# Two graph-attention layers on one core: the statistics of the last batch, one count, and the last normalization are moved

## The chip, the cores and the metric

The kernel runs on one core of one Trainium2 chip. The metric is the device time of one execution in microseconds (us): 3082.63 in the median of three runs, 3081.44 to 3082.72.

## The reference

For x of 16 x 1024 x 256 (float32) and 16 adjacency matrices of 1024 x 1024, two layers follow one another. Each layer normalizes, projects, attends under the mask of the adjacency matrix, projects back and adds to x:

```python
h = jnp.maximum(_layernorm(x), 0.0)
q, k, v = h @ Wq, h @ Wk, h @ Wv        # per head; layer 1 adds biases
scores = jnp.where(adj > 0, q @ k.T / sqrt(D), -inf)
heads = softmax(scores) @ v
x = x + concat(heads) @ Wo.T + bo
```

Layer 0 has 4 heads of 64 columns, layer 1 has 8 heads of 32.

## The kernel before

**Steps.** For one batch and one layer the queries are cut into two halves of 512 (`qh`), the heads into two groups (`g`), and the keys into tiles of 128. A *group* is one `qh` and one `g`; its work is a list of *steps*. A step computes four blocks of scores of 128 keys x 512 queries (`scores`), which fill two PSUM pairs. VectorE applies the mask while it reads each pair (`exponentials`, L562), ScalarE takes the exponential in place (L568), and two steps later (`LEAD`) TensorE multiplies the values by them (`weigh`, L580) into the PSUM tile `po`. A layer 0 group has 4 steps and a layer 1 group has 8. So a batch is 16 steps of layer 0 and 32 of layer 1, 768 steps over all batches. Layer 0 of batch b+1 stands before layer 1 of batch b. The text calls the first step of layer 1 of batch 14 (the last but one) c, as the code does; e = c + 32 is the first step of layer 1 of batch 15, and e + 31 is the last step of all.

**Sums.** The softmax needs the sum of the exponentials over the keys. In layer 1 GpSimd adds the tiles of an odd step to those of the even step before it (`count_steps`, L695, two adds). Accumulating DMAs on GpSimd's queue (`accumulate`, L681) add such tiles to each other. `count` (L425) then lets TensorE add over the partitions, with a matrix of ones, into the PSUM tile `pz`, which exists once. `halves` does a count as two counts of 256 columns in two following steps. After it `spread` (L445, L458) copies the sums to SBUF, into a tile of the tag inv, and sends them by four DMAs to a tile of 128 partitions; `invert` (L466, L468) takes reciprocals and writes them to DRAM; `fetch` (L477) reads them back, spread over partitions, into tiles of the tag inv, of which there are two; `normalize` (L485, GpSimd) multiplies the heads' output `cat`, which `copy_out` (L437, ScalarE) copied from `po`. `end_half` (L521, L526) multiplies by Wo and adds to x.

**Inputs of a layer.** `stats` (L198 and L199 on VectorE, then four small operations on GpSimd, L209 to L212) gives mean and variance of the four row tiles of a half; `norm` (L221, ScalarE) writes the normalized rows into the one tile of the tag hn; `add_bias` (L230, GpSimd) adds the output bias to x beforehand. `turn_blocks` (L273) transposes blocks of 32 x 32 on VectorE; `put_blocks` (L278) writes them to DRAM and `place_blocks` (L285, four DMAs) reads them back into hT. The products `k`, `q` (L307) and `values` (L383) read hT; each takes one of the three PSUM pairs that the scores use as well. ScalarE moves k and the values out of PSUM and VectorE moves q (L322).

**Order.** The order of every queue is the order in which `Stream.run` issues the work. It goes through the steps; `later(i, f, ...)` puts a piece of work into step i by hand. In a step come: the scores, the weighted values of the step two before, counts, the exponentials with the copies of finished groups between their halves, other due work in the order in which it was entered, and last the large products. At an even step of layer 1 that holds a large product, the weighted values are put off to the next step. `Group.waits` gives the step of a group's final count, counted from its end, and `end_group` the steps of spread, invert, fetch and normalize.

**The ends.** In the last 32 steps (`pairs`) every pair of steps is counted by itself. The last group (`hurry`) is counted at once, and `finish` ends the kernel: products of its half with Wo for the group before (L496), reciprocals of the sums straight from PSUM in two halves (L505), multiplication of `cat` by them (L506), the other products, the addition to x (L511) and the output DMAs (L514). `test` (L333, L336, GpSimd) then checks the sums' range; a reduction (L953) and a tiny product (L955) of its result follow, and a flag is read that selects a second program for inputs out of range.

Of the kernel before, what the change touches and what calls it, by code (L numbers as in the profile page):

```python
# [10 lines left out]
F32 = mybir.dt.float32  # L11
# [7 lines left out]
P = 128  # L19
# [71 lines left out]
def fast_program(ctx, tc, a, w, loads, chk):  # L91
# [5 lines left out]
    B, N, E = x.shape  # L97
    NT = N // P
# [5 lines left out]
    work = ctx.enter_context(tc.tile_pool(name="work", bufs=2))  # L104
# [288 lines left out]
    class Group:  # L393
# [93 lines left out]
        def finish(self):  # L487

            inp, qh = self.inp, self.qh
            inv = work.tile([P, 512], F32, tag="inv", name=f"inv_{self.n}")  # L490
            py = psum_pair(f"py_{self.n}").rearrange("p a (t e) -> p (a t) e", e=E)
            rows, cat = xs[inp.b, qh], self.half.cat
            dst = quarters(out, inp.b, qh)

            def product(i, c):
                nc.tensor.matmul(  # L496
                    py[:, i, :], cat[:, c, ts(i, P)], w.o[self.layer][:, c, :],
                    start=c == 0 and i % 2 == 0, stop=c == 1 and i % 2 == 1,
                )

            for i in range(4):
                product(i, 0)
            for h in range(2):
                q = ts(h, 256)
                nc.vector.reciprocal(tiled(inv)[:, ts(h, 2)], by_tile(self.s)[:, ts(h, 2)])  # L505
                nc.vector.tensor_mul(cat[:, self.g, q], cat[:, self.g, q], inv[:, q])  # L506
                for i in (2 * h, 2 * h + 1):
                    product(i, 1)
            for h in range(2):
                t = ts(h, 2)  # L510
                nc.vector.tensor_add(rows[:, t, :], py[:, t, :], rows[:, t, :])  # L511
                for g in range(4):
                    queue = nc.scalar if g % 2 else nc.sync
                    queue.dma_start(dst[g][:, t, :], rows[ts(g, 32), t, :])  # L514
# [91 lines left out]
    class Stream:  # L606
# [12 lines left out]
        def later(self, i, f, *args):  # L619
            self.due.setdefault(i, []).append((f, args))  # L620
# [5 lines left out]
        def run(self):  # L626
            steps = self.steps
            n = len(steps)
            waiting, i = [], 0
            while i < n + LEAD:  # L630
                wide = 2 if i < n and steps[i].gr.layer == 0 else 1
                span = range(i, i + wide)
                now = [steps[k] for k in span if k < n]
                waiting += [(k, steps[k - LEAD]) for k in span if k >= LEAD]
                for st in now:
                    scores(st)
                copies = []
                if wide == 2 or i % 2 or not self.large(i):
                    ahead = [st for _, st in waiting if st.gr.hurry and st.j >= NT - 2]
                    for _, st in waiting:  # L640
                        if st not in ahead:
                            weigh(st)
                    for k, st in waiting:
                        if st.gr.layer:
                            self.count_steps(k, st)
                        if st in ahead:
                            weigh(st)
                        if st.last:
                            copies.append(st.gr.copy_out)
                            self.end_group(k, st.gr)  # L650
                    waiting = []
                due = [self.due.pop(k, []) for k in span]

                for f, args in [e for of in due for e in of]:
                    if f.__name__ in COUNTS:
                        f(*args)
                for st in now:
                    exponentials(st, copies if wide == 1 else [])
                if not now:
                    for f in copies:  # L660
                        f()
                for k, of in zip(span, due):
                    if wide == 2 and k % 2:
                        for f in copies:
                            f()
                    if k % 2 and 3 <= k <= n and steps[k - 2].gr.layer == 0:
                        add_tiles(steps[k - 3], steps[k - 2])
                    for f, args in of:
                        if f.__name__ not in COUNTS and not self.rank((f, args)):
                            f(*args)  # L670
                for of in due:
                    for f, args in of:
                        if self.rank((f, args)):
                            f(*args)
                i += wide
            while self.due:
                for f, args in self.due.pop(min(self.due)):
                    f(*args)
# [4 lines left out]
        def count_steps(self, i, st):  # L683


            gr, j = st.gr, st.j
            if gr.hurry and j >= NT - 2:
                if st.last:
                    self.counted(i, gr)
                gr.count([of[:, r, :] for of in st.halves for r in range(2)], False, st.last)  # L690
            elif j % 2:
                one = self.steps[i - LEAD - 1].p
                for k, of in enumerate(st.halves):
                    half = one[:, ts(k, 2), :]
                    nc.gpsimd.tensor_add(half, half, of)  # L695
                if gr.pairs and (st.last or gr.hurry):
                    self.later(i + 2, gr.count, one, j == 1, st.last)
                elif gr.pairs:
                    self.halves(i + 3, gr, one, j == 1, False)
                elif j == 1:  # L700
                    gr.one = one
                elif gr.brief:
                    if j == 3:
                        self.accumulate(one, gr.one)
                        self.later(i + 6, gr.count, one, True, False)
                    elif j == 5:
                        self.halves(i + 5, gr, one, False, False)
                    else:
                        self.later(i + 4, gr.count, one, False, True)
                elif j == 5:  # L710
                    gr.two = one
                elif st.last and gr.qh and not gr.g:
                    self.accumulate(one, gr.two)
                    for k, of in enumerate((gr.one, one)):
                        self.later(i + gr.waits, gr.count, of, not k, k == 1)
                elif st.last and gr.last:
                    self.accumulate(gr.two, gr.one)
                    self.later(i + 1, self.accumulate, one, gr.two)
                    self.later(i + gr.waits, gr.count, one, True, True)
                elif st.last:  # L720
                    self.accumulate(gr.two, gr.one)
                    self.later(i + 2, self.accumulate, one, gr.two)
                    if gr.g:
                        self.halves(i + gr.waits, gr, one, True, True)
                    else:
                        self.later(i + gr.waits, gr.count, one, True, True)
                else:
                    self.accumulate(one, gr.one)
                    gr.one = one
# [12 lines left out]
        def end_group(self, i, gr):  # L742

            if gr.hurry:
                for f in (gr.spread, gr.finish, gr.inp.test):
                    self.later(i, f)
                return

            if gr.layer == 0:
# [5 lines left out]
                at = (3, 4, 5, 7, 13) if gr.qh else (3, 5, 6, 7, 11)  # L755
                if gr.inp.b == B - 1 and gr.qh:
                    at = 3, 6, 7, 9, 13
                if gr.inp.b == 0:
                    at = (2, 3, 4, 5, 8) if gr.qh else (3, 5, 6, 7, 9)
            else:  # L760
                at = ((9, 11, 13, 19), (8, 12, 14, 17, 19), (7, 9, 11, 14), None)[2 * gr.qh + gr.g]
                if gr.pairs:
                    at = 2, 5, 6, 7, 9
                elif gr.last:
                    at = 4, 6, 7, 9, 11
            for k, f in zip(at, (gr.spread, gr.invert, gr.fetch, gr.normalize)):
# [87 lines left out]
    later = stream.later  # L854
# [34 lines left out]
    for t in range(NT):  # L889
        i = 7 + 2 * t  # L890
# [8 lines left out]
    for b in range(B - 1):  # L899
# [32 lines left out]
                later(a + at[t + 1] + (1 if t == 4 else 2), mask.flip, t)  # L932
        else:
            last, e = inputs[1][b + 1], c + 32
            later(c + 5, last.stats, 0)
            later(c + 10, last.norm, 0)
            later(c + 13, last.add_bias, 0)
            block_inputs(last, 0, c + 11, c + 12, c + 13, c + 18, c + 22, c + 26)
            later(c + 18, last.stats, 1)
            later(c + 22, last.norm, 1)  # L940
            later(c + 23, last.add_bias, 1)
            block_inputs(last, 1, c + 23, c + 24, c + 26, e, e + 10, e + 2)
            for i, u in zip((4, 10, 14, 26, 36, 40, 42, 44), range(NT)):
                later(c + i, masks[b + 1].second, u)
    stream.run()

# [247 lines left out]
```

## Time and profile before

| what | us |
|---|---|
| median of three runs | 3082.63 |
| profiled execution, its own time | 3083.88 |
| its span, first to last instruction | 3082.1 |
| TensorE busy | 3061.3 |
| VectorE busy | 2464.4 |
| ScalarE busy | 2242.9 |
| GpSimd busy | 2462.1 |

PE is TensorE, PEld its weight loads, DVE VectorE, ACT ScalarE, POOL GpSimd, SP the queue of SyncE that issues most DMAs (SPq). A line of the timeline has the start, the time to the end of its last instruction, the engine, the line of the code, the operation, the output and inputs by the program's names, and the number of instructions merged in it; in brackets stands how long the engine idled before, and what ended that. A matmul of the program counts as two in the trace. A line of the windows has the stretch, its length, busy time and instructions of PE, PEld, DVE, ACT and POOL, the clock that TensorE was granted (1.00 is full), the share of the DMA engines in use, and GB/s.

### The profile page before, as it was taken

What the parts mean: (1) busy time and instruction counts of PE and PEld (TensorE: products, weight loads), DVE (VectorE), ACT (ScalarE), POOL (GpSimd) and SP (SyncE); (2) the same over time, 40 slices, a digit from 0 to 9 for tenths busy, and PEclk for the clock granted to TensorE, in tenths of its full rate; (3) what the DMA queues carried; (4) which work ended last, traced back from release to release, by engine and by line L of the source; (5) the groups of instructions that cost most, each with busy time, mean ns of one, the idle gap of its engine ahead of it and who ended that gap; (6) DMA issues with size and microseconds to landing.
All of it is one profiled execution on the core that took longest, in us unless ns stands there. A gap on an engine that the chain in (4) does not pass through costs nothing.

```text
span 3082.1 us, 46012 instructions
## 1 busy us (share of the span) xinstructions
PE 3061.3 (99%) x16678; PEld 1199.8 (39%) x16678; DVE 2464.4 (80%) x2712; ACT 2242.9 (73%) x2478; POOL 2462.1 (80%) x1584
## 2 busy tenths in 40 slices
PE   9999999999999999999999999999999999999998
PEld 4443433434334343343433334343343433434333
DVE  6778787887878878787887878878788787887877
ACT  5668777777777767777777777777777777776775
POOL 3578788787887878878788887888878778787886
PEclk9999999999999999999999999999999999999999
DMA  4226556464563645546456463654636546463431
GB/s 134 63 61 147 129 123 135 121 141 121 129 145 110 139 130 133 136 110 138 124 129 138 120 139 108 147 123 122 141 104 144 132 122 138 118 143 86 100 82 34
DMA packets 263548, 372.77 MB, mean 121 GB/s; under 512 B 58768, under 2 KB 218768, under 8 KB 242448
## 3 DMA queue, kind: packets, MB, share of 16 engines
q0 software_dynamic: 23472, 170.93, 28.2%
q1 hardware_dynamic: 239520, 198.56, 22.2%
q8 instruction: 133, 2.18, 0.3%
q14 instruction: 103, 0.84, 0.1%
q10 hardware_dynamic: 320, 0.26, 0.0%
HBM read 149.95 MB, written 47.96 MB: 64 GB/s over the span
## 4 chain that ended last, share of the span: by engine, by line
PE 92%; DVE 2%; DMA 2%; POOL 1%; issue 1%; SPq 1%; ACT 1%; DVEq 0%; ACTq 0%; POOLq 0%
PE ps L539 31%; PE po L580 28%; PE pq L307 10%; PE py L521 7%; PE pv L383 6%; PE pq L348 5%; PE pz L425 4%; PE pv L367 2%; DVE p L562 1%; DMA p<-p 1%; POOL p L695 1%; DMA sums<-s 0%; DMA inv<-vd 0%; ACT p L568 0%; SPq L458 0%
## 5 line engine op out<-in xcount | busy, mean ns | idle before, releaser
L562 DVE SCALAR_TENSOR_TENSOR p<-mask,ps 128x1024 f32<-128x1024 fp8e5 x1536 | 1791.6, 1215 | 346.0 <-PE ps L539 327.2
L568 ACT ACTIVATE p<-p 128x1024 f32<-128x1024 f32 x1536 | 1615.9, 1056 | 597.1 <-DVE p L562 535.4
L695 POOL TENSOR_TENSOR p<-p,p 128x1024 f32<-128x1024 f32 x510 | 1218.1, 2472 | 104.9 <-PE po L580 104.3
L539 PE MATMUL ps<-qT,kT 32*128 32x512 f32 (+1 forms) x6144 | 1089.9, 629 | 5.5 <-DVE p L562 3.5
L580 PE MATMUL po<-p,v 128*32 128x512 f32 (+1 forms) x6144 | 967.9, 599 | 0.4 <-ACT cat L437 0.4
L539 PEld LDWEIGHTS ps<-qT,kT 32*128 32x128 f32 (+1 forms) x6144 | 355.4, 184 | 640.2 <-DVE p L562 269.5
L580 PEld LDWEIGHTS po<-p,v 128*32 128x32 f32 (+1 forms) x6144 | 239.4, 118 | 669.7 <-issue 498.6
L593 POOL TENSOR_TENSOR p<-p 128x1024 f32<-128x1024 f32 x128 | 302.8, 2366 | 79.4 <-DVE p L592 74.1
L592 POOL TENSOR_TENSOR p<-p,p 128x1024 f32<-128x1024 f32 x64 | 151.2, 2363 | 157.3 <-DVE p L589 128.9
L485 POOL TENSOR_TENSOR cat<-cat,inv 128x512 f32<-128x512 f32 x127 | 175.2, 1383 | 77.7 <-DMA inv<-vd 76.5
L521 PE MATMUL py<-wo,cat 128*128 128x256 f32 x1008 | 234.4, 386 | 0.0
L521 PEld LDWEIGHTS py<-wo,cat 128*128 128x128 f32 x1008 | 186.3, 190 | 73.5 <-issue 16.7
L681 POOL DMA_DIRECT2D p<-p x163 | 144.8, 889 | 86.5 <-DMA p<-p 55.2
L383 PE MATMUL pv<-wv,hT 128*128 128x256 f32 x800 | 185.7, 385 | 0.0
L307 PE MATMUL pq<-hT,wq 128*128 128x512 f32 x400 | 184.8, 605 | 0.1
L167 ACT ACTIVATE mask<-adj,numbers 128x1024 fp8e5<-128x1024 int32 x128 | 145.9, 1140 | 45.0 <-DMA adj<-in_adj_dram 45.0
L383 PEld LDWEIGHTS pv<-wv,hT 128*128 128x128 f32 x800 | 148.0, 190 | 57.1 <-issue 25.2
L589 DVE TENSOR_TENSOR p<-p 128x1024 f32<-128x1024 f32 x128 | 166.9, 1304 | 0.0
L526 DVE TENSOR_TENSOR x<-py,x 128x1024 f32<-128x1024 f32 x63 | 77.1, 1224 | 109.1 <-PE py L521 109.1
L437 ACT COPY cat<-po 128x512 f32<-128x512 f32 x128 | 73.7, 576 | 118.5 <-PE py L521 96.6
L595 POOL TENSOR_TENSOR p<-p,p 128x1024 f32<-128x1024 f32 x64 | 151.9, 2373 | 5.0
L230 POOL TENSOR_TENSOR x<-x,bo 128x1024 f32<-128x1024 f32 x64 | 155.7, 2503 | 0.0
(71 smaller groups left out, 1961.2 us busy)
## 6 DMA issues: line engine op xcount, KB each, us to landing
p<-p POOLq DMA_DIRECT2D x163, 1024.0 KB, 7.9
adj<-in_adj_dram SPq DMA_DIRECT2D x512, 128.0 KB, 3.0
turned<-hn SPq DMA_DIRECT2D x58, 512.0 KB, 3.6
hT<-turned SPq DMA_DIRECT2D x232, 128.0 KB, 2.9
x<-in_x_dram SPq DMA_DIRECT2D x128, 128.0 KB, 3.0
inv<-vd SPq DMA_DIRECT2D x128, 128.0 KB, 3.0
inv<-vd SPq DMA_DIRECT2D x252, 64.0 KB, 2.5
out_dram<-x SPq DMA_DIRECT2D x124, 128.0 KB, 2.2
```

What stands on the lines that cost most here:

```text
L230: nc.gpsimd.tensor_add(rows, rows, w.bo[self.layer].unsqueeze(1).to_broadcast([P, 4, E]))
L307: nc.tensor.matmul(pq[:, m, :], wt[self.layer][:, c, ts(m, P)], self.hT[half][:, c, :], start=(c == 0), stop=(c == 1),)
L383: nc.tensor.matmul(pv[:, i, :], self.hT[half][:, c, ts(i, P)], w.v[self.layer][:, c, :], start=(c == 0), stop=(c == 1),)
L485: nc.gpsimd.tensor_mul(o, o, inv)
L521: nc.tensor.matmul(py[:, i, :], self.half.cat[:, c, ts(i, P)], w.o[self.layer][:, c, :], start=(c == 0), stop=(c == 1),)
L539: nc.tensor.matmul(st.ps[i // 2][:, i % 2, :], gr.inp.kT[r * D : (r + 1) * D, gr.g, ts(kt, P)], gr.inp.qT[gr.qh][r * D : (r + 1) * D, gr.g ...
L562: nc.vector.scalar_tensor_tensor(out=half, in0=gr.mask.m[gr.qh][:, kt // 4, :, kt % 4].unsqueeze(1).to_broadcast([P, 2, 512]), scalar=-EDG ...
L568: nc.scalar.activation(half, half, AF.Exp, scale=gr.scale)
L580: nc.tensor.matmul(gr.o[r * D : (r + 1) * D, :], gr.inp.v[:, kt, h * D : (h + 1) * D], st.halves[i // 2][:, i % 2, :], start=(kt == 0), st ...
L589: nc.vector.tensor_add(a, a, b)
L593: nc.gpsimd.tensor_add(a, a, b)
L695: nc.gpsimd.tensor_add(half, half, of)
```

## The change

It consists of five parts.

1. For layer 1 of batch 15, the statistics of half 0 go from step c+5 to c+10, the normalization from c+10 to c+14, the addition of the bias from c+13 to c+15, the block transpose, its put and its place from c+11, 12, 13 to c+15, 16, 17, and the product of k from c+18 to c+20. The products of q and of the values stay at c+22 and c+26.
2. The statistics of half 1 go from c+18 to c+20, and the third piece of the mask's second form (`second`, L178) from c+14 to c+20.
3. In layer 1 of batch 14, the first of the two counts of group `qh` = 1, `g` = 0 is done in halves, three and four steps after the group's end instead of whole after six.
4. In layer 1 of batch 15, the group before the last has its reciprocals, fetch and normalization one step earlier.
5. In `finish`, the reciprocals go to a tile of the tag hn instead of inv. The last group's `spread` is issued ahead of its `copy_out`, with the copies, instead of behind it.

```diff
-            inv = work.tile([P, 512], F32, tag="inv", name=f"inv_{self.n}")
+            inv = work.tile([P, 4 * E], F32, tag="hn", bufs=1, name=f"inv_{self.n}")[:, :512]
...
                         if st.last:
+                            if st.gr.hurry:
+                                copies.append(st.gr.spread)
                             copies.append(st.gr.copy_out)
                             self.end_group(k, st.gr)
...
                     self.accumulate(one, gr.two)
-                    for k, of in enumerate((gr.one, one)):
-                        self.later(i + gr.waits, gr.count, of, not k, k == 1)
+                    if gr.inp.b == B - 2:
+                        self.halves(i + 3, gr, gr.one, True, False)
+                    else:
+                        self.later(i + gr.waits, gr.count, gr.one, True, False)
+                    self.later(i + gr.waits, gr.count, one, False, True)
...
             if gr.hurry:
-                for f in (gr.spread, gr.finish, gr.inp.test):
+                for f in (gr.finish, gr.inp.test):
                     self.later(i, f)
                 return
...
                 if gr.pairs:
-                    at = 2, 5, 6, 7, 9
+                    at = (2, 4, 5, 6, 9) if gr.qh else (2, 5, 6, 7, 9)
...
-            later(c + 5, last.stats, 0)
-            later(c + 10, last.norm, 0)
-            later(c + 13, last.add_bias, 0)
-            block_inputs(last, 0, c + 11, c + 12, c + 13, c + 18, c + 22, c + 26)
-            later(c + 18, last.stats, 1)
+            later(c + 10, last.stats, 0)
+            later(c + 14, last.norm, 0)
+            later(c + 15, last.add_bias, 0)
+            block_inputs(last, 0, c + 15, c + 16, c + 17, c + 20, c + 22, c + 26)
+            later(c + 20, last.stats, 1)
...
-            for i, u in zip((4, 10, 14, 26, 36, 40, 42, 44), range(NT)):
+            for i, u in zip((4, 10, 20, 26, 36, 40, 42, 44), range(NT)):
                 later(c + i, masks[b + 1].second, u)
```

## The prediction

> **What bounds the kernel now.** I read the page first, then TensorE's waits, the timeline of each engine around the steps that the change names, the windows there for the clock, and the last 25 us.
>
> ```profile
> PE 3061.3 (99%) x16678; PEld 1199.8 (39%) x16678; DVE 2464.4 (80%) x2712; ACT 2242.9 (73%) x2478; POOL 2462.1 (80%) x1584
> ```
>
> TensorE is busy 99%, but the ends of matmuls are modelled, so short stalls hide in long ones. Every edit lies in the last 215 us. Counting score groups gives step c at 2847.24, c+5 2869.97, c+7 2874.96, c+10 2885.52, c+14 2898.64, c+18 2911.06, c+20 2919.88, c+22 2924.38, e = c+32 2957.79.
>
> TensorE's timeline at c+7, VectorE's before it, and windows with the granted clock (the column before the last two):
>
> ```profile
> 2874.96 1.13 PE L539 MATMUL ps<-qT,kT 32*128 32x512 f32 x4
> 2877.32 1.13 PE L539 MATMUL ps<-qT,kT 32*128 32x512 f32 x4 [1.23 <-DVE p L562]
> 2878.37 1.92 PE L580 MATMUL po<-p,v 128*32 128x512 f32 x8
> ...
> 2873.48 0.42 DVE L198 BATCH_NORM_STATS2 st<-x 128x6 f32<-128x256 f32 x1
> ...
> 2876.07 4.58 DVE L562 SCALAR_TENSOR_TENSOR p<-mask,ps 128x1024 f32<-128x1024 fp8e5 x4
> ...
> 2878.50:2879.00 0.50, 0.50 (x4) 0.06 (x5) 0.50 (x1) 0.50 (x1) 0.50 (x2) 0.50 1.27 262
> 2881.00:2881.50 0.50, 0.50 (x8) 0.00 (x0) 0.00 (x0) 0.50 (x1) 0.50 (x1) 0.50 1.26 262
> ```
>
> The statistics at c+5 hold VectorE 2.6 us, the scores of c+7 find no free PSUM pair, TensorE stands idle 1.23 us, and then runs at half clock from about 2878.5 to 2881.7. This is the stall that the first edit can remove. Right behind it stands GpSimd:
>
> ```profile
> 2877.23 0.89 POOL L681 DMA_DIRECT2D p<-p  x1 [0.30 <-POOL p L695]
> 2877.89 0.47 POOL L209 TENSOR_TENSOR ve<-mv,numbers 128x4 f32<-128x4 f32 x1
> ...
> 2879.73 9.36 POOL L695 TENSOR_TENSOR p<-p,p 128x1024 f32<-128x1024 f32 x4
> ...
> 2911.49 3.48 DVE L562 SCALAR_TENSOR_TENSOR p<-mask,ps 128x1024 f32<-128x1024 fp8e5 x3 [0.27 <-POOL p L695]
> ```
>
> From 2872.24 to 2929.8 GpSimd pauses about 2 us in all, and at 2911.49 VectorE waits for it. At the end one chain decides:
>
> ```profile
> 3066.50 0.58 ACT L437 COPY cat<-po 128x512 f32<-128x512 f32 x1 [2.90 <-PE po L580]
> 3066.68 1.26 POOL L485 TENSOR_TENSOR cat<-cat,inv 128x512 f32<-128x512 f32 x1 [3.05 <-DMA inv<-vd]
> 3067.60 2.41 SPq L458 DMA_DIRECT2D sums<-s  x4
> 3067.98 1.76 DVE L505 RECIPROCAL inv<-pz 128x256 f32<-128x256 f32 x1 [5.47 <-POOL cat L485]
> 3071.33 0.33 POOL L333 TENSOR_SCALAR held<-sums 128x32 f32<-128x32 f32 x1 [1.89 <-DMA sums<-s]
> 3073.55 1.29 DVE L511 TENSOR_TENSOR x<-py,x 128x512 f32<-128x512 f32 x2 [0.48 <-PE py L496]
> ```
>
> The reciprocal of the last sums waits for a normalization that has nothing to do with them: it takes over that one's inv buffer.
>
> **Part 1, statistics of half 0 from c+5 to c+10.** Durations from the rows: a step's two masked scores 2.27 on VectorE (six instructions in 6.88, the last 1.21), a plain step on TensorE 2.0 (scores 1.07, weighted values 0.93), an odd step's two adds on GpSimd 4.7. Three PSUM pairs and two buffers per odd half give the links: a score pair, or a large product, needs the pair three before it read; an odd step's halves need the adds of four steps before. Without the statistics VectorE ends c+5 at 2873.5, c+6 at 2875.85, c+7 at 2878.1, a small reciprocal 0.2, c+8 at 2880.55. GpSimd, without its four small operations (1.84), starts the adds of c+5 at 2877.9 and ends them at 2882.5; the second half of c+9 waits for that and ends at 2883.7. So the product of q at c+10 starts at 2883.75, not 2886.86: 3.1 us won.
>
> Most of it is given back. At c+10 VectorE ends its scores at 2885.97, the statistics (2.67) at 2888.6; they hold the q evictions (1.41) to 2890.0, two before the old 2892.0. GpSimd has added c+7 by 2887.2 and issued its DMA by 2888.1, waits for the statistics, and does the small operations (1.62 in their second row) to 2890.25. Behind them are queued layer 0's normalizations (2.51), to 2892.8, and the adds of c+9, which start 0.15 us before the old 2892.96 and end at 2897.5. The second half of c+13 needs those, ends at 2898.7, and frees the pair for the output product of c+14: 2898.75 against 2899.98. **1.2 us** is left there.
>
> **Part 2, the steps behind it.** The bias add (2.4 to 2.7) goes from before to after the adds of c+13. These now wait for weights at c+15, 2904.4, and end at 2909.1; bias to 2911.5, adds of c+15 to 2916.2 (old 2915.8). The transpose (1.24) follows c+15's scores, 2905.9 to 2907.1. By the links c+19 ends at 2917.4, so the product of k, now at c+20, starts at 2917.45, and q at c+22 at 2925.1 against 2926.50: **1.4 us**. The second statistics (2.67), moved under the product of k at c+20, lie in VectorE's wait for it. From 2932.43 GpSimd works without a real pause to 2957.4, and c+31 waits for it (1.13), so the 1.4 us should reach e. The normalization on ScalarE (four in 2.06) follows c+14's exponentials, 2902.05 to 2904.1, 1.8 before the transpose needs it, in time where ScalarE idled 1.81. The mask's second half on ScalarE (1.13) now stands before the copy of kT: that ends at 2923.3, 0.7 us before scores need the pair.
>
> **Part 3, DMAs.** Nothing is added, but the room shrinks. In the SP timeline, and in the landing of the placing line there:
>
> ```profile
> 2895.45 0.33 SPq L278 DMA_DIRECT2D turned<-hn  x1
> 2898.10 4.34 SPq L285 DMA_DIRECT2D hT<-turned  x4
> ...
> DMA to landing us min/median/max: 7.0/8.0/8.2
> ```
>
> They land at about 2909, and k starts at 2913.3: 4 us of room. Now they are put at 2907.1; with 2.6 to 4.7 for the put, 2.4 to 4.3 for four issues and 2.6 to 9.7 for the last landing (all seen after 1000 us), hT is there between 2914 and 2924. The lower end holds with no accumulating DMA beside it. By the walk one ends at 2911.3 (2903.5 plus 7.8) and the next starts at 2916.5, so I take the low side: about 2917, cost **0**, ends 0 and 6. On the same queue stand next the sums of group 0 (2916.56 before); VectorE waited 0.59 for them then, and now does the statistics first, so I charge nothing.
>
> **Part 4, halves.** Two counts of 0.6 at c+28 and c+29 replace one of 1.0 at c+31. At c+28 VectorE waits 0.50 for scores, so the halves would be exposed, but it waits 0.49 and 1.13 for GpSimd right after. I take **0**; ends -1.0 (gone from c+31) and +1.1 (both bare). The first sum's DMA, issued at 2929.8, has landed long before.
>
> **Part 5, the end.** The inverse of group 2 moves up a step: reciprocal at 3057.05 (VectorE idles until 3057.80), vd landed 1.44 later plus issue, inv by 3064.0 with the old 3.1 and 2.1. GpSimd's adds end at 3063.6, normalization at 3065.4: before the last weighted values, 3066.45. The reciprocal in the hn buffer, whose last reader was the put at 2935.09, waits for the counts only, 3065.4 to 3067.15; product with cat 3067.6 (copied 3066.50 to 3067.08; the sums' copy ahead fills 3065.45 to 3066.05, while ScalarE idled, so costs nothing). Second reciprocal 3069.35, product 3069.8, last matmuls 3070.95, against 3073.51. Then the check is late: the four DMAs of the sums start at 3066.1, reach GpSimd 3.73 later as before, 3069.83; two tests (1.51) and the reduction give 3071.6, and VectorE does that before its output adds. These start at 3071.6 instead of 3073.55: **1.9 us**. Bounds: 1.0, if only one DMA step is gained, and 2.6, if the adds come first.
>
> **Sum.** -1.4 + 0 + 0 - 1.9 = -3.3 us: the profiled execution, 3083.88 (span 3082.1), becomes 3080.6; it stands 1.25 above the median 3082.63, which becomes **3079.3**.
>
> **Clock.** The row: 1.23 us idle, then some 3.2 us at half clock, at 2877. My walk leaves new gaps before the products of c+10 (1.45), c+14 (1.85) and c+20 (1.35). In the Trainium skill, TensorE: Matmul & The Clock Gate, section What's actually happening, the clock is halved only after at least one idle window of about 3.4 us; by that these gaps would cost nothing more, and the row, shorter than that and yet halved, speaks against it. By the row each can cost 3.2/2 = 1.6; gaps of 1.1 hidden at c+13 and c+22 kept full clock. I keep it out of the sum and make it a rival.
>
> **Rivals.**
> - GpSimd does not hold the steps back, and all that c+5 lost stays won: c+10 at 2881.0 instead of 2885.52, 4.5, with the end 1.9: **3076.2**, range 3074 to 3077.5. For: no wait for GpSimd shows before 2911. Against: its unbroken row.
> - New gaps halve the clock twice: +3.2, **3082.5**. For: the row. Against: a gap is read from a walk that may be 0.5 off.
> - Slower: hT is late. Place: the product of k at c+20. Price: a last landing of 9.7 means 2923, 5.6 behind 2917.4, and one half clock 1.6: 3079.3 + 7.2 = **3086.5**. It decides from an hT at 2920.8 on, where the 3.3 are eaten. For: 8 us landings at the old place; against: the window between two accumulating DMAs.
> - The middle edits only trade places: the end alone, 3080.7, inside my own range of 3078 to 3081.
>
> **How the numbers follow.** My forecast 0.42, the full gain 0.26, half clocks 0.17, late hT 0.15. A measurement can tell about 0.2%, 6.2 us: faster means below 3076.5, slower above 3088.8. Of the full gain 0.18 lies below 3076.5, of the late hT 0.06 above 3088.8 (q and the queue behind it held too); the rest is the same. The range leaves out 0.08 below 3075 and 0.1 above 3085.
>
> **What would show it.** Right: no idle TensorE near c+7 and full clock there; q at c+10 about 3 us earlier against step c, at c+22 1.4; the last reciprocals waiting for counts and cat ready before the last weighted values. Wrong: a wait of k on hT<-turned at c+20, half clock after c+10, c+14 or c+20, or GpSimd idle where I have it bind.

## The result: 5.8 us slower, and the profile after

The changed kernel takes 3088.69 us in the median, the kernel before 3082.89 on the same chip: a ratio of 1.0019, with a 95% interval of 1.0011 to 1.0027. The forecast was 3079.3, range 3075 to 3085. The profiled execution took 3090.17 (span 3088.4), 6.29 more than the one before. The page hardly shows where: TensorE is busy 3.5 us more, partly because slower matmuls count as busy, and the other engines as long as before within 1 us:

```profile
PE 3064.8 (99%) x16686; PEld 1204.1 (39%) x16686; DVE 2463.5 (80%) x2712; ACT 2243.1 (73%) x2478; POOL 2461.9 (80%) x1584
```

The steps before c are the same in all kernels here, yet c itself starts between 2845.3 and 2848.2 in their profiles. So the pieces are counted from c, each in the one profiled execution of its kernel: to the start of the product of k at e, from there to the start of the last weighted values, and from there to the output addition (L511).

| us | c | c to k at e | to last weighted values | to addition | sum from c |
|---|---|---|---|---|---|
| before | 2847.24 | 111.62 | 106.44 | 8.25 | 226.31 |
| after | 2847.53 | 118.21 | 107.46 | 6.67 | 232.34 |
| difference | 0.29 | +6.59 | +1.02 | -1.58 | +6.03 |

The end won nearly what was forecast. The middle, forecast to win 1.4, lost 6.6.

**c+5 to c+10, as forecast.** TensorE's timeline at c+7 and the windows there (length, then busy time of PE, PEld, DVE, ACT, POOL, then the granted clock) of the changed kernel:

```profile
2875.24 1.51 PE L539 MATMUL ps<-qT,kT 32*128 32x512 f32 x8
2876.68 1.06 PE L580 MATMUL po<-p,v 128*32 128x512 f32 x8
...
2878.50:2879.00 0.50, 0.50 (x10) 0.06 (x8) 0.50 (x2) 0.43 (x2) 0.50 (x1) 1.00 0.00 0
2881.00:2881.50 0.50, 0.50 (x8) 0.16 (x8) 0.50 (x2) 0.43 (x2) 0.50 (x1) 1.00 0.55 115
```

The four scores of c+7 follow one another without the 1.23 us of idle time, and the clock stays full. The product of q at c+10 starts 36.98 after c, before it was 39.62: 2.6 won, where 3.1 were forecast.

**c+14, against the forecast.** TensorE's timeline goes on like this, and these are the windows behind it:

```profile
2884.51 3.70 PE L307 MATMUL pq<-hT,wq 128*128 128x512 f32 x8 [0.87 <-DVE p L562]
...
2896.10 1.13 PE L539 MATMUL ps<-qT,kT 32*128 32x512 f32 x4
2901.23 2.08 PE L539 MATMUL ps<-qT,kT 32*128 32x512 f32 x4 [4.00 <-DVE p L562]
2903.54 5.83 PE L521 MATMUL py<-wo,cat 128*128 128x256 f32 x16 [0.24 <-DVE p L562]
...
2901.00:2902.00 1.00, 0.77 (x2) 0.50 (x4) 0.17 (x1) 0.79 (x1) 1.00 (x1) 0.51 0.00 0
2904.00:2906.00 2.00, 2.00 (x6) 1.55 (x6) 1.75 (x2) 1.85 (x3) 2.00 (x2) 0.50 0.96 197
```

TensorE idles 4.00 us inside c+14 and comes back at half clock: the output product takes 5.83 instead of the 3.72 before. The scores of c+14 start 2.8 earlier than before, counted from c; the product behind them ends 5.4 later. What it waited for is told by the chain of waits (start, length, what), cut to four of its long pieces:

```profile
2879.15 7.64 DMA vd<-vn
...
2888.66 7.57 DMA inv<-vd
...
2897.58 4.66 POOL p L697 x2
...
2902.26 1.23 DVE p L562
```

The inverse sums of layer 0's last half (written to vd, read back as inv) come late. The timelines of SP and GpSimd have the place and the other thing that was under way, and the view of the reads (L477) their time to landing:

```profile
2886.86 2.40 SPq L477 DMA_DIRECT2D inv<-vd  x4
2887.54 1.12 POOL L683 DMA_DIRECT2D p<-p  x1
...
2890.98 1.27 POOL L485 TENSOR_TENSOR cat<-cat,inv 128x512 f32<-128x512 f32 x1
2896.36 1.26 POOL L485 TENSOR_TENSOR cat<-cat,inv 128x512 f32<-128x512 f32 x1 [4.11 <-DMA inv<-vd]
2897.58 4.65 POOL L697 TENSOR_TENSOR p<-p,p 128x1024 f32<-128x1024 f32 x2
...
DMA to landing us min/median/max: 2.9/4.3/7.6
```

The same views of the kernel before:

```profile
2886.32 2.40 SPq L477 DMA_DIRECT2D inv<-vd  x4
2889.03 0.89 POOL L681 DMA_DIRECT2D p<-p  x1
2890.48 2.51 POOL L485 TENSOR_TENSOR cat<-cat,inv 128x512 f32<-128x512 f32 x2 [0.56 <-DMA inv<-vd]
...
DMA to landing us min/median/max: 2.9/3.1/3.5
```

In the kernel before, GpSimd issued its accumulating DMA of c+9 at 2889.03, after the four reads of inv, and these landed 2.9 to 3.5 us after their issue. Now GpSimd, free of the statistics, issues it at 2887.54, in the middle of the four (the last is issued at 2888.66), and the last of them takes 7.6. The write to vd was late too: it took 7.64, before 5.41, beside the accumulating DMA of c+5, so that, counted from c, the reads start 0.25 later than before although the reciprocal ahead of them (L466) came 2.0 earlier. GpSimd is in order: the second normalization waits 4.11 us, the adds of c+9 stand behind it, the exponentials of c+13 need the buffer that those adds read, and the product of c+14 needs the PSUM pair that they free.

**c+20.** Two smaller waits are new or longer. They stand in the timelines of VectorE and GpSimd of the changed kernel, and then of the kernel before:

```profile
2930.88 0.25 DVE L466 RECIPROCAL vn<-sums 128x16 f32<-128x16 f32 x1 [1.45 <-DMA sums<-s]
...
2931.13 0.87 POOL L683 DMA_DIRECT2D p<-p  x1 [2.33 <-DMA p<-p]
```

```profile
2923.99 0.25 DVE L466 RECIPROCAL vn<-sums 128x16 f32<-128x16 f32 x1 [0.59 <-DMA sums<-s]
...
2923.88 0.90 POOL L681 DMA_DIRECT2D p<-p  x1
```

The second accumulating DMA of group 1 (`qh` = 0, `g` = 1) needs the first one landed. Before, the four small operations of the statistics and two adds stood between the two on GpSimd; now the small operations come behind the second, and GpSimd idles. VectorE waited 0.59 for the sums of group 0 (`qh` = 0, `g` = 0) before, and 1.45 now.

**The end.** The timelines of ScalarE, SP, VectorE and GpSimd over the last 9 us:

```profile
3073.61 0.58 ACT L445 COPY s<-pz 128x512 f32<-128x512 f32 x1 [2.21 <-PE pz L425]
3074.22 2.41 SPq L458 DMA_DIRECT2D sums<-s  x4
3074.23 1.76 DVE L505 RECIPROCAL inv<-pz 128x256 f32<-128x256 f32 x1 [3.92 <-ACT s L445]
3077.95 0.33 POOL L333 TENSOR_SCALAR held<-sums 128x32 f32<-128x32 f32 x1 [3.27 <-DMA sums<-s]
3079.54 0.19 DVE L958 TENSOR_REDUCE row<-chk 128x1 f32<-128x32 f32 x1 [0.89 <-POOL chk L336]
3079.87 1.29 DVE L511 TENSOR_TENSOR x<-py,x 128x512 f32<-128x512 f32 x2
```

The reciprocal no longer waits for a normalization, as forecast. The check of the sums (L333 to L958), forecast as the last thing before the additions, ends at 3079.72; but the chain that ended last goes through the two reciprocals, and its last products with Wo end at 3079.83, 0.1 later. The first reciprocal does not start when the counts are done, at 3073.52: it starts 0.03 after ScalarE has copied the sums, though both only read `pz`. In the Trainium skill, page PSUM — Partial Sum Buffer, section PSUM bank collisions raise a hardware error, the compiler's scheduler is said to order any two instructions of different engines that touch the same bank and quadrant, reads too; the row agrees.

### The profile page after: what moved, and what is told of

Read it like the earlier page. It is cut to its first block, busy times and chain, and to the rows that moved or that the text cites. A ratio compares the mean times of both kernels' runs of the same rounds, so it can differ in the third digit from the quotient of the medians.

```text
span 3088.4 us, 46027 instructions
## 1 busy us (share of the span) xinstructions
PE 3064.8 (99%) x16686; PEld 1204.1 (39%) x16686; DVE 2463.5 (80%) x2712; ACT 2243.1 (73%) x2478; POOL 2461.9 (80%) x1584
## 3 DMA queue, kind: packets, MB, share of 16 engines
q8 instruction: 133, 2.18, 0.3%
## 4 chain that ended last, share of the span: by engine, by line
PE 89%; DMA 3%; DVE 3%; POOL 2%; issue 1%; SPq 1%; ACT 1%; DVEq 0%; POOLq 0%; ACTq 0%
PE ps L539 30%; PE po L580 27%; PE pq L307 9%; PE py L521 7%; PE pv L383 6%; PE pq L348 4%; PE pz L425 4%; PE pv L367 2%; POOL p L697 2%; DVE p L562 1%; DMA p<-p 1%; DMA vd<-vn 1%; DMA inv<-vd 1%; DMA sums<-s 0%; POOL cat L485 0%
```

## The experiments

The table has the same pieces for every run, and the time against the kernel before in runs on the same chip. In it, "q" is the start of the product of q at c+10, and "k" that of k at e.

| kernel | c to q | c to k | to last weighted | to addition | sum | median, us, against before | ratio, 95% interval |
|---|---|---|---|---|---|---|---|
| before | 39.62 | 111.62 | 106.44 | 8.25 | 226.31 | | |
| after | 36.98 | 118.21 | 107.46 | 6.67 | 232.34 | +5.80 | 1.0011 to 1.0027 |
| e1, middle only | 36.96 | 117.83 | 106.88 | 7.94 | 232.65 | +6.15 | 1.0010 to 1.0028 |
| e2, end only | 38.54 | 111.37 | 106.69 | 6.66 | 224.72 | -1.79 | 0.9985 to 1.0003 |
| e3, one DMA out | 36.97 | 113.75 | 107.65 | 6.65 | 228.05 | +1.01 | 0.9994 to 1.0012 |
| e4, early inverse | 36.96 | 113.81 | 107.80 | 6.66 | 228.27 | +1.66 | 0.9994 to 1.0012 |
| e5, e4 + fill | 36.96 | 112.08 | 106.39 | 6.65 | 225.12 | -0.81 | 0.9987 to 1.0005 |
| e6, e5 + late inverse | 36.98 | 112.07 | 106.33 | 6.65 | 225.05 | -0.94 | 0.9986 to 1.0005 |
| e9, e5 + late DMA | 36.98 | 111.87 | 106.35 | 6.65 | 224.87 | -0.20 | 0.9990 to 1.0008 |
| e12, e6 + e9 | 36.98 | 110.76 | 106.34 | 6.65 | 223.75 | -2.88 | 0.9981 to 0.9999 |
| e7, halves only | 38.53 | 110.93 | 107.07 | 8.20 | 226.20 | +2.14 | 0.9999 to 1.0017 |
| e10, the same again | 38.54 | 110.95 | 107.40 | 8.21 | 226.56 | +1.30 | 0.9997 to 1.0015 |
| e8, e2 + fill at c+7 | 38.53 | 111.08 | 106.35 | 6.65 | 224.08 | -1.61 | 0.9986 to 1.0005 |
| e11, e8 + early inverse | 38.54 | 111.11 | 106.52 | 6.65 | 224.28 | -0.61 | 0.9988 to 1.0007 |

A verdict on one or two us rests on the trace's pieces, since the medians scatter by about one us. The pieces have a scatter of their own: e7 and e10 are the same kernel, and their sums differ by 0.36.

### e1 and e2: the middle alone, the end alone

e1 makes parts 1 and 2 on the kernel before, e2 parts 4 and 5.

```diff
 e1
-            later(c + 5, last.stats, 0)
...
+            later(c + 10, last.stats, 0)
...
 e2
+            inv = work.tile([P, 4 * E], F32, tag="hn", bufs=1, name=f"inv_{self.n}")[:, :512]
...
+                                copies.append(st.gr.spread)
...
+                    at = (2, 4, 5, 6, 9) if gr.qh else (2, 5, 6, 7, 9)
```

> Parts 1 and 2 alone (statistics, normalization, transpose, put, place and k of batch 15, and the mask piece) on the kernel before. Theory A: the loss lies wholly here. GpSimd is free 1.5 us earlier at c+9, issues the accumulating DMA then, its data run into the last of the four inv fetches, GpSimd waits 4.1 us for that before its second normalization, and TensorE stands 4.0 us at c+14 and runs 3.2 us at half clock after it (2.1 lost): about +7.5 us against before, 3090.4, with the same wait of 4 us. Theory B (the halved count or the end cost time): below +4 us, 3087 or less.

> Parts 4 and 5 alone (earlier inverse, hn buffer, sums copied first) on the kernel before. From the trace after, the addition to x starts 6.67 us behind the last weighted values' group start, against 8.25 before: -1.6 us, 3081.3. The prediction had -1.9. Theory B: no gain or a loss.

e1 alone is 6.15 slower in the median and +6.3 in the pieces, 6.2 of it before k at e; its TensorE waits 3.80 in c+14 and its GpSimd 3.9 for inv. So the loss belongs to parts 1 and 2. e2 wins 1.6 in the last piece and 1.79 in the median.

e2 showed one more thing that bears on the clock. Its c+7 is untouched and has the old gap, but not the old half clock behind it. TensorE's timeline and a window of e2:

```profile
2876.61 1.13 PE L539 MATMUL ps<-qT,kT 32*128 32x512 f32 x4 [1.23 <-DVE p L562]
...
2879.00:2880.00 1.00, 1.00 (x12) 0.24 (x12) 1.00 (x2) 0.93 (x2) 1.00 (x2) 1.00 1.28 262
```

Its product of q at c+10 therefore starts 1.1 earlier than in the profile of before, with nothing changed there. Of the 2.6 that the change seemed to win at c+10, only 1.56 are the edit's, measured against e2. At c+14 nothing is left of them: the output product there starts 51.65 after c in e2, and 51.9 in e4 and e5, which have the statistics moved and no late inv.

### e3 and e4: is it the collision?

The theory after e1: the accumulating DMA beside the reads of inv makes them late. e3 leaves that one DMA out of the changed kernel; e4 keeps it and lets the reciprocal and the reads start a step earlier.

```diff
 e3
-                    self.accumulate(gr.two, gr.one)
+                    if not (gr.inp.b == B - 2 and not gr.qh and not gr.g):
+                        self.accumulate(gr.two, gr.one)
 e4
-                    at = 3, 6, 7, 9, 13
+                    at = 3, 5, 6, 9, 13
```

> The whole change, but the accumulating DMA issued at c+9 (group 0 of layer 1 of batch 14, its first one after the last step) is left out, so that group's sums lack the first four steps. Theory A: with nothing to run into, the last inv fetch lands about 3 us after its issue, no 4 us wait of GpSimd, no gap of TensorE at c+14 and full clock there: 6 us less than the whole change, 3082 to 3083 or a little less, as GpSimd saves an issue too. Rival C (the statistics ahead of the normalizations, or GpSimd's later load, hold the steps back): still 3086 or more.

> The whole change, with the inverse and fetch of layer 0's last half of batch 15 one step and two steps earlier (c+6 and c+7 instead of c+7 and c+8). The inverse is then written before the accumulating DMA of c+5 moves and fetched well before that of c+9. Theory A: no wait at the normalization, no gap at c+14: 6 us or more less than the whole change, 3080 to 3082.5. Rival C: 3086 or more, with TensorE's gap at c+14 left over 2 us.

Both take the 4 us wait away: in e3 GpSimd's two normalizations run as one block, from 2889.52, and in e4 from 2891.05, without a wait. The view of e3's reads (L477):

```profile
DMA to landing us min/median/max: 3.0/3.1/3.1
```

So the DMA of c+9 is what makes the reads late. In e4 they run beside that of c+5 instead and take 6.7 to 9.3, but start so early that they land before GpSimd needs them. Against the changed kernel the pieces win 4.3 and 4.1, where the theory asked for 6. It was the late inv, but not alone. Both are still 1.7 to 2.0 behind the kernel before. TensorE's timeline and a window of e4 show what is left:

```profile
2896.17 2.18 PE L539 MATMUL ps<-qT,kT 32*128 32x512 f32 x8
2899.54 5.41 PE L521 MATMUL py<-wo,cat 128*128 128x256 f32 x16 [1.19 <-DVE p L562]
...
2902.00:2903.00 1.00, 1.00 (x4) 0.82 (x3) 0.00 (x0) 1.00 (x2) 1.00 (x1) 0.50 1.26 262
```

The scores take 2.18 instead of 1.07, so about 1.1 us of waiting is hidden in them, another 1.19 is seen before the product, and then the clock is halved and the product takes 5.41. e3 has the same rows (1.20 and 5.41).

### e5: fill the gap

Four spare matmuls of 128 x 128, whose result nobody reads, stand in e4's gap.

```diff
+    def fill(n):
+        spare = ps_o.tile([P, 512], F32, tag="pz", name="spare")
+        for _ in range(n):
+            nc.tensor.matmul(spare[:, :P], w.ident, w.ident, start=True, stop=True)
...
+            later(c + 14, fill, 4)
```

> The run before this one (whole change, earlier inverse), with four spare products of 128 x 128 (about 0.3 us each, into the count's free PSUM tile, read by nobody) in TensorE's gap ahead of the output product of c+14. The work of the kernel is the same. Theory D (the gap itself is what halves the clock): the gap of 1.2 us is filled, the product takes 3.7 us instead of 5.4 at full clock, and the kernel gains about 1.7 us: 3083.3. Rival E (the half clock comes from the large product, or the stall is too long anyway): clock still 0.5 in the product, no gain, or a loss of up to 1.

TensorE's timeline of e5, and a window in the product:

```profile
2896.53 1.16 PE L864 MATMUL spare<-ident 128*128 128x128 f32 x8
2897.80 3.72 PE L521 MATMUL py<-wo,cat 128*128 128x256 f32 x16
...
2900.00:2902.00 2.00, 2.00 (x16) 1.30 (x14) 0.45 (x2) 1.96 (x4) 2.00 (x1) 1.00 0.95 197
```

The product starts where it did in e4 (51.9 after c) and takes 3.72 at full clock: k at e comes 1.73 earlier than in e4. (The sum wins 3.15; the other 1.4 lie behind e and go with a write of vd that is no longer late, told under Part 4 below.) The half clock at c+14 was real and cost that. Still, k at e stands 0.46 behind before, though the product of c+14 starts 0.83 ahead of it: something between c+14 and e gives back 1.3.

### e6, e9 and e12: what gives it back

Two things were new at c+20: GpSimd's idle 2.3 and VectorE's longer wait for sums. e6 puts group 0's inverse a step later; e9 issues group 1's second accumulating DMA a step later, so that the small operations come ahead of it; e12 does both.

```diff
 e6
-                at = ((9, 11, 13, 19),
+                at = ((9, 12 if gr.inp.b == B - 2 else 11, 14 if gr.inp.b == B - 2 else 13, 19),
 e9
-                    self.later(i + 2, self.accumulate, one, gr.two)
+                    late = gr.inp.b == B - 2 and not gr.qh and gr.g
+                    self.later(i + (3 if late else 2), self.accumulate, one, gr.two)
```

> As the last, and the inverse and fetch of group 0 of layer 1 of batch 14 one step later (c+21 and c+23 instead of c+20 and c+22). Theory F: the sums, sent at c+18, land 6.5 us late beside the accumulating DMA of c+19; VectorE then no longer waits 1.5 us for them ahead of the scores of c+21, and the product of q at c+22 starts about 1.1 us earlier: 1 us below the last run. Rival: the wait is hidden behind the product of k, no gain (within 0.3).

> As e5 (whole change, earlier inverse, gap ahead of the output product of c+14 filled), and the second accumulating DMA of group 1 one step later, at c+20, so that on GpSimd the four small operations of the second statistics stand ahead of it and not behind. Theory G (what is left to lose in the middle is GpSimd's chain: it idles 2.3 us there, waiting for the accumulating DMA before, since the small operations that used to fill that wait were moved behind it): the wait is filled, the accumulating DMA of c+29 is issued about 1.6 us earlier against the start of step c, and so is e: 3079.8. Rival H (e is set by TensorE and VectorE): no change, 3081.4.

> The steps of e6 and e9 together: whole change, earlier inverse, filled gap at c+14, group 0's inverse one step later, and group 1's second accumulating DMA one step later. Each alone gave nothing at e: with the first, GpSimd still idled 2.3 us for a DMA; with the second, VectorE still waited 1.4 us for sums and GpSimd 1.3 us for the weighted values behind them. Theory G: both stand at the same place, and only both gone give time: the accumulating DMA of c+29 comes 1.0 to 1.3 us earlier against step c than in e9 (110.86), the kernel 3080 to 3080.5 where before stands at 3082.2. Rival H: TensorE and VectorE set e, nothing won, 3081.3 or more.

Alone, each does nearly nothing at e: 112.07 and 111.87 against 112.08. In e6 the product of q at c+22 does come 1.1 earlier (78.54 after c, not 79.68), and GpSimd's wait remains; in e9 GpSimd's wait is gone and VectorE still waits 1.43 for sums. GpSimd's timelines of e5 and of e12 at this place:

```profile
2923.30 0.87 POOL L683 DMA_DIRECT2D p<-p  x1 [2.31 <-DMA p<-p]
```

```profile
2929.61 0.87 POOL L683 DMA_DIRECT2D p<-p  x1 [0.30 <-POOL p L697]
2930.71 4.70 POOL L697 TENSOR_TENSOR p<-p,p 128x1024 f32<-128x1024 f32 x2 [0.23 <-PE po L580]
```

In e12 GpSimd's adds at 2930.71 wait only 0.23 for weighted values; in e9 they wait 1.33, with VectorE's wait still there. So two engines, each in order, held the steps, and either wait by itself was enough. Together they give 1.3: k at e comes at 110.76, 0.86 before the old one. e12 takes 3080.53 us against 3083.41 on the same chip, with an interval just below 1. Its pieces are 0.86 ahead of before in the middle and 1.6 at the end. But the profile of before has the half clock at c+7. Against e2, e8 and e11, which have the old middle and full clock there, e12's k at e is only 0.3 to 0.6 ahead, and against e7 and e10 0.2. So it is shown that the repairs take the loss away, and not that the moved statistics win more than a few tenths.

### e7 and e10: the halves alone

Part 3 alone, twice.

> Part 3 alone (the first count of group 2 in halves at c+28 and c+29) on the kernel before. The prediction had 0, between -1.0 and +1.1. The stretch from c+26 to e was 0.7 us shorter with the whole change, so -0.7 if that carries through to the end; 0 if GpSimd's adds at c+31 set e anyway.

> Part 3 alone once more, the same kernel as e7. Its median was 2.1 us above before, while its trace shows the same length from c to the end within 0.1. If the loss is of the kernel, +2 again; if it was scatter of those runs, within 0.8 of before. From the trace I expect 0.

k at e comes 0.7 earlier than in before. The full clock at c+7 (q 1.1 earlier) is part of that: e2, with the same clock and without part 3, has 0.25. Between e and the last weighted values 0.6 and 1.0 go back, with a late write of vd (told under Part 4 below). The pieces say -0.1 and +0.25. The medians say +2.1 and +1.3, with intervals that hold 1. The profiled execution of e7 was the fastest of its eleven (3082.06, median 3084.34), so its trace can't show what the others lost. This stays open: part 3 costs between nothing and 2 us.

### e8 and e11: the old gap filled

e8 puts five spare matmuls into the gap of c+7 of e2; e11 adds e4's earlier inverse.

```diff
+            if i == 2 and gr.layer and gr.inp.b == B - 2 and not gr.qh and not gr.g and st.j == 7:
+                fill(5)
```

> The kernel before with parts 4 and 5 (the end), and five spare products of 128 x 128 between the two score pairs of c+7, where TensorE waits 1.23 us because of the statistics, which stay at c+5. Theory D: the gap stays but is filled, the clock stays full from 2878.5 to 2881.7, and of the 1.6 us of matmul time lost there about 1 to 1.6 come back against the run with the end only: 3080 to 3080.5. Rival E: half clock all the same; 3081.5 or more.

> As e8 (the kernel before with the end and spare products at c+7), and the inverse and fetch of layer 0's last half one and two steps earlier. In e8 the clock was full and yet nothing was gained at e, as GpSimd's chain sets it; GpSimd no longer waits there for inv (0.6 us before, 0 in e8). Theory G: nothing more to win, 3080.6 within 0.5. Rival H: TensorE's waits at the product of c+10 go, 1 us gained.

e8 was meant to price the half clock at c+7. It could not: e2 already had full clock there, and both have q at 38.5. Against e2, e8 has the same q and 0.6 less in the sum, within scatter. e11 adds nothing to e8 (111.11 against 111.08 at e): with the statistics at their old place there was nothing to win from an earlier inverse.

## Why the prediction was wrong, point by point

**Part 1 failed, and decided.** The failed step is "layer 0's normalizations (2.51), to 2892.8". It counts the normalizations' own time and takes their input as there, because before it was. Measured, the second waits 4.11 us, and the adds behind them start at 2897.58. The working had both numbers that make the collision: it moved GpSimd's DMA from 2889.03 to about 2887, and the reads of inv stood at 2886.3 to 2888.1. It looked for DMAs that the change moves by hand (part 3), and not for one that moves because the engine that issues it comes free. The rest of the walk came out 0.4 late: without the collision the product of c+14 starts 51.9 after c (e4, e5), and the walk said 51.5. But its gain of 1.2 was measured against a profile with the half clock at c+7. e2, e7 and e8, with the statistics at c+5 and full clock, have 51.65, so the move wins nothing there.

**The clock was a rival and belonged into the sum.** The forecast named c+14 as one of three gaps that can cost 1.6; e5 measured 1.73. The other two, before the products of c+10 and c+20, cost nothing: these take 3.70 each. The rival gave 3082.5, and alone it would not have reached the result.

**Of the 1.2 at c+14, nothing reaches e** without the edits of e12: in e5 the product of c+14 is 0.83 ahead of before, and k at e 0.46 behind. Even in e12 the product of q at c+22 is 0.7 ahead of before, where 1.4 were forecast. The failed step is in part 2: that GpSimd "works without a real pause", so a gain is carried. Moving the second statistics uncovers 2.3 us of GpSimd's wait for its own DMA, which their small operations had covered.

**Part 3, DMAs, "I charge nothing"** for the sums behind the hT transfers: VectorE waits 1.45 there, 0.86 more than before. It is not the hT transfers that hold them: the first two of the four landed 1.7 after their issue, and the other two, beside the accumulating DMA issued at 2923.28, 4.7 and 6.5 after theirs. The rival that hT is late did not come true: the places, issued from 2917.98 on, landed 2.8 to 2.9 after their issue, the last at 2922.71, 1.9 before k at 2924.64.

**Part 4, the halves, 0 us:** -0.1 and +0.25 by the pieces; open by the medians. In the changed kernel 1.02 is lost between e and the last weighted values. There a count waits for its weights, and takes 2.61 instead of 1.57. The weight loads and matmuls of the changed kernel:

```profile
3033.96 0.14 PEld L425 LDWEIGHTS pz<-p,ones 128*32 128x32 f32 x4 [1.00 <-POOL p L697]
...
3032.41 2.61 PE L425 MATMUL pz<-p,ones 128*32 128x256 f32 x16
```

GpSimd's adds come 1 us late for it, since the normalization ahead of them waits for its inv; in GpSimd's timelines of the changed kernel and of before:

```profile
3027.96 1.27 POOL L485 TENSOR_TENSOR cat<-cat,inv 128x512 f32<-128x512 f32 x1 [1.76 <-DMA inv<-vd]
```

```profile
3020.05 1.28 POOL L485 TENSOR_TENSOR cat<-cat,inv 128x512 f32<-128x512 f32 x1 [0.71 <-DMA inv<-vd]
```

The write of vd took 3.3 there, and 1.4 in before. e3, e4, e7 and e10 have it late as well (2.9 to 3.3), and e5, e6, e9 and e12, with part 3 too, have not (1.8 to 2.2): so it is not part 3 as such. What goes with it in all 14 traces is one transfer of 16 KB on the queue that loads instructions (q8). Where it starts 0.8 to 1.2 after the write is issued, the write takes 2.9 to 3.3; where it starts up to 0.3 ahead of it, 1.8 to 2.4; where it starts after the write has landed, 1.4. No run moves that transfer alone, so this is read from the traces and not shown by an experiment.

**Part 5 was right but for its size:** 1.6 instead of 1.9. The mis-sized term is the first reciprocal, put right behind the counts; it also waits for ScalarE's copy, 0.6, and the counts end 0.2 later than the walk had them. So the last products, put 0.65 ahead of the check, end 0.1 behind it.

**The sum:** +6.6 (middle) + 1.0 - 1.6 = +6.0, where -3.3 was forecast. Of the 9.3 between them the middle makes 8.0. The forecast's range ended at 3085 and its slowest rival, a late hT, at 3086.5; none let the reads of inv collide.

## What to carry to other kernels

When work is taken off an in-order engine, everything behind it on that engine moves earlier, its DMAs too: lay each new issue time against the transfers of other queues, above all against one whose result the same engine waits for next. An operation that seems to be in the way may be what covers a wait; before moving it, ask what the instruction behind it will then wait for. And where two engines each hold a step, undoing one shows nothing: an edit without effect is tried again together with the other. Last, one profile of the old kernel can hold a stall, as the half clock at c+7, that its other executions do not have: a gain is measured against more than one.

## What the runs showed of the hardware

- Small transfers issued beside an accumulating DMA (GpSimd's queue, 128 x 2048 floats, 1 MB) land two to five times later: reads of inv 7.6 us instead of 2.9 to 3.5, the write of vd 7.6 (1.4 at the end of the kernel, with none beside it). e3 shows it for inv by leaving that DMA out. In the changed kernel those held back landed 0.2 behind it: inv at 2896.23 and the DMA at 2896.07, vd at 2886.80 and the DMA at 2886.59. One that is issued right behind it can still be quick: a write of vd 0.39 after the DMA of 2923.88 landed in 1.4 (before). The accumulating DMA itself takes 6.8 to 10.2.
- The half clock comes in stretches of 3.41 us: one in before, e3 and e4, two in a row in after (2901.03 to 2907.85) and e1. In each trace all changes of the clock lie a whole number of 3.413 apart (in before the two of c+7 by 1, and the fall at the end, 3076.41, by 57 from the second), on a grid that lies elsewhere in each execution. These are windows on that grid, of before and then of e2, counted back from the fall at its end (3074.02):

```profile
2875.03:2878.44 3.41, 2.18 (x12) 0.59 (x16) 3.31 (x7) 1.07 (x2) 3.11 (x4) 1.00 0.00 0
2878.44:2881.85 3.41, 3.41 (x17) 0.64 (x16) 2.38 (x3) 3.16 (x3) 3.33 (x4) 0.50 1.06 219
```

```profile
2872.63:2876.04 3.41, 2.75 (x20) 0.46 (x12) 3.17 (x10) 1.25 (x2) 3.41 (x2) 1.00 0.01 1
2876.04:2879.46 3.42, 2.85 (x20) 0.97 (x20) 3.42 (x4) 2.73 (x3) 3.04 (x7) 1.00 0.56 115
```

- A gap of 1.2 us halves the clock in one place and not in another. In before the gap of c+7 lies within one stretch, which has 2.18 of matmuls, and the next is halved; in e2 the grid cuts the gap in two, and the clock stays full. At c+14 such a gap, with about as much hidden just before, halved the clock in both kernels that had it (e3, e4, 2.2 of matmuls in the stretch ahead), and in none of the four where spare matmuls filled it. But in e7 and e10 the gap of c+7 lies within one stretch too, with 2.2 of matmuls, and the clock stays full, so where the line runs is open. The Trainium skill, TensorE: Matmul & The Clock Gate, section What's actually happening, says that the window by which the hardware judges is free-running, so that the point of change depends on where in it the work lands; the grid agrees. Its idle window of about 3.4 us has the length of these stretches, but those ahead of the half clock in before, e3 and e4 were not idle, and there the measurement decides: such a gap can cost 1.7 us, half a stretch.
